# Mixture of experts: the weights of the routes travel with the scattered rows, and the gathers add to x by themselves

## The chip, the cores and the metric

The kernel runs on one core of a Trainium2 chip. A core has a matrix engine (PE, with a queue of its own for loading weights, PEld), a vector engine (DVE), a scalar engine (ACT), GpSimd (POOL) and SyncE (SP); SP and POOL issue the data transfers (DMAs) here, which run on 16 DMA engines. The metric is the device time in microseconds (us) of one execution. Lower is better.

## The reference

The model has two pre-norm transformer blocks over 8 sequences of 512 tokens with 256 features each, in float32:

```
x = x + attn0(layernorm(x));  x = x + ffn0(layernorm(x))
x = x + attn1(layernorm(x));  x = x + ffn1(layernorm(x))
```

- attn0: 16 query heads over 4 key and value heads of 16 features, rotary positions, causal. attn1: 16 heads of 16 with biases, causal.
- ffn0: a router picks 8 of 32 experts for each token, with the softmax weights divided by their sum over the eight; ffn1: 2 of 16, with the softmax weights as they are, plus a shared expert of inner width 352 for every token. An expert is `h = silu(x @ wg) * (x @ wu)`, and the token's result adds `(h @ wd) * w_e`. The inner width is 96 in ffn0 and 176 in ffn1.

Since the weight w_e is one number for a token and an expert, `(h @ wd) * w_e` and `(h * w_e) @ wd` are the same up to rounding.

## The kernel before

A token's row of x lives in a tile `x` of 128 partitions with 4 x 256 floats: token 128 t + p of a sequence is on partition p in part t. Only four such tiles are in the core's memory at once, so between its stages a sequence's x goes out to DRAM (`x_after`, L161) and is fetched again (`fetch_x`, L164).

**Order of the stages.** Attention 0 over the eight sequences (0 to 676 us of the profile), layer 0's experts (676 to 1172), attention 1 (1172 to 1768), layer 1's experts (1768 to 2003), and a tail that puts out the last three sequences (2003 to 2056). In the attention stages a sequence's layer norm (L289), router (`route`, L313) and, in layer 1, the shared expert run beside the attention of the next one (`pipeline`, L743).

**Sorting by expert.** For each layer and part of the sequences (layer 0: sequences 0 to 3 and 4 to 7; layer 1: 0 to 4 and 5 to 7) DRAM holds a slab `xg` (L222) with room for each expert's tokens one after the other. `route` finds each token's experts, its weights `wt` (one column for each expert, zero where it isn't chosen, L350 to L357) and its row in each chosen expert's part of the slab. An indirect DMA on POOL for each t and each of the k choices then scatters 128 normed rows of 256 floats (L384): 32 for a sequence in layer 0, and 8 in layer 1. Three wide DVE instructions after them (L394, L397, L399) bring the weights into the order of the choices, as `lay.weights`.

**Experts.** `tables` (L980) works out, at run time, which tiles of 128 rows there are and to which expert each belongs; `registers` (L1076 to L1096) reads that into registers of SP (where a tile's rows begin) and PE (where the expert's weights lie), eight tiles at a time. `experts` (L1068) then runs over pairs of tiles, 150 in layer 0 and 44 in layer 1, in five stages with lags of 0, 4, 5, 6 and 7 steps (L1172): load the rows (L1106, six buffers), transpose them on PE and copy to xT (L1115, L1117), the gate and up products with silu on ACT and one multiply on DVE (L1132, L1137 to L1141), transpose h (L1151, L1152), the down product (L1162), a copy on ACT (L1167) and a store into a second slab `yg` (L1168). PE's order is the one in which the program writes it (L1173). The other engines' order within their queues is set by a scheduler of the framework.

**Gathers.** When all tiles of a part are stored, indirect DMAs on POOL gather a token's results from `yg` (L1199), 32 for a sequence in layer 0 and 8 in layer 1, 128 rows of 256 floats each. They land in a ring of four tiles of two gathers each (`AHEAD`, `PART`), and for each of them DVE computes x = g * weight + x (`add`, L1210). The gathers of layer 0's sequences 0 to 3 run beside the second part of its experts (`x_in_ring`, L1366), and those of 4 to 7 beside attention 1, two sequences ahead (`ahead1`, L1438). In layer 1, sequences 0 to 4 are gathered and put out beside the second part (`results`, L1279), and 5 to 7 in the tail, with a ring of eight tiles. `Beside` (L1046) hands such work out between the steps of the experts. `behind` orders an add after DVE's latest copy of an expert's h, or after the latest mask in attention 1, so that adds don't overtake these.

Of the kernel before, what the change touches and what calls it, by code (L numbers as in the profile page):

```python
# [72 lines left out]
AHEAD = 4  # L73
# [18 lines left out]
def two_blocks_kernel(  # L92
# [56 lines left out]
    zeros = cpool.tile([P, D], F32, tag="zeros", name="zeros")  # L149
# [60 lines left out]
    class Layer:  # L210
        def __init__(self, n, part, seqs, n_e, k, gu):
# [10 lines left out]
            self.xg = drp.tile([n_e * self.cap + P, D], F32, tag=f"xg{name}", name=f"xg{name}")  # L222
# [16 lines left out]
            self.weights = routes("weights", k, F32)  # L239
# [41 lines left out]
    def layernorm(x, lnp, name, tag="xn", bufs=1):  # L281
# [7 lines left out]
        xn = lnp.tile([P, NT, D], F32, tag=tag, name=f"xn_{name}", bufs=bufs)  # L289
        for t in range(NT):  # L290
            nc.vector.tensor_scalar(
                xn[:, t, :], x[:, t, :], mv[:, t, 0:1], rstd[:, t : t + 1], ALU.subtract, ALU.mult
            )
# [18 lines left out]
    def ffn_parts(smp, bank):  # L312
        def route(n, b, xn, xT, name, again):  # L313
# [36 lines left out]
            wt = smp.tile([P, NT, n_e], F32, tag="wt", name=f"wt_{name}")  # L350
# [31 lines left out]
            for t in range(NT):  # L382
# [7 lines left out]
            yield  # L390

            same = smp.tile([P, NT, k, n_e], F32, tag="same", name=f"same_{name}", bufs=1)
            shape = [P, NT, k, n_e]
            nc.vector.tensor_tensor(  # L394
                same, key.unsqueeze(2).to_broadcast(shape), keys[:, :, :k].unsqueeze(3).to_broadcast(shape), ALU.is_equal
            )
            nc.vector.tensor_tensor(same, same, wt.unsqueeze(2).to_broadcast(shape), ALU.mult)  # L397
            weights = lay.weights[b]
            nc.vector.tensor_reduce(weights, same, AX.X, ALU.add)  # L399
# [580 lines left out]
    def tables(lay, small, bank, again, beside=None):  # L980
# [3 lines left out]
        lay.offi = tpool.tile([1, 2, most], I32, tag=f"offi{lay.part}", name=f"offi{name}")[:, :, :n_t]  # L984
# [41 lines left out]
        offf = small.tile([1, 2, n_t], F32, tag="offf", name=f"offf_{name}", bufs=1)  # L1026
        dn = D if lay.n == 0 else ND1 * D
        nc.vector.tensor_scalar(offf[:, 0, :], ex, float(n_e - 1), float(lay.gu), ALU.min, ALU.mult)
        nc.vector.tensor_scalar(offf[:, 1, :], ex, float(n_e - 1), float(dn), ALU.min, ALU.mult)
# [3 lines left out]
        for lo in range(0, n_e, 8):  # L1033
            with tc.issue_after(beside.load) if beside else ExitStack():
# [5 lines left out]
                for rows in at:  # L1040
                    inst = nc.sync.dma_start(out=lay.xg[rows, :], in_=zeros)
                    tc.declare_no_dep(inst.ins, group=group, reason="these rows are no token's")
                    tc.add_to_no_dep_group(group, inst.ins)
            yield

    class Beside:  # L1046


        def __init__(self, *items):
# [3 lines left out]
            self.last = None  # L1053
# [17 lines left out]
    def experts(n, gu, dn, mp, ps, again, beside):  # L1071
# [10 lines left out]
        def registers(lay, i):  # L1082
# [7 lines left out]
                    lay.offi[0:1, j, i : min(i + RB, lay.tiles(again))], engines=[ENG.PE], min_val=0, max_val=(lay.n_e - 1) * step,  # L1090
                    skip_runtime_bounds_check_because="an expert's number is at most the last one's",
                )[1]
                for j, step in enumerate((lay.gu, w_dn))
# [6 lines left out]
        def load(lay, i):  # L1100
# [3 lines left out]
            xg = mp.tile([P, 2, D], F32, tag="xg", name=f"xg_{name}_{part}_{i}", bufs=6)  # L1104
# [4 lines left out]
        def turn_x(lay, i):  # L1109
            part = lay.part  # L1110
            xg = made.pop(("xg", part, i))
# [8 lines left out]
        def gate_up(lay, i):  # L1120
            part = lay.part
            xT = made.pop(("xT", part, i))
# [4 lines left out]
            else:  # L1127
                gus = [ps.tile([P, 2 * inner], F32, tag="gu", name=f"gu_{name}_{part}_{i + j}") for j in range(2)]
            for j in range(2):
# [6 lines left out]
                if n:  # L1136
                    nc.scalar.activation(h[:, j, :], gus[j][:, :inner], AF.Silu)  # L1137
                    nc.vector.tensor_tensor(h[:, j, :], h[:, j, :], gus[j][:, inner:], ALU.mult)
            if n == 0:
                nc.scalar.activation(h, whole[:, :, :inner], AF.Silu)  # L1140
                nc.vector.tensor_tensor(h, h, whole[:, :, inner:], ALU.mult)  # L1141
            made["h", part, i] = h

        def turn_h(lay, i):
# [7 lines left out]
            beside.last = nc.vector.tensor_copy(hT[: chunks[0][1]], hp[: chunks[0][1]]).ins  # L1152
# [28 lines left out]
    PART = 2  # L1181

    def gathers(n, b, gat, again=""):
# [11 lines left out]
        for t in range(NT):  # L1195
            for lo in range(0, k, PART):
                g = gat.tile([P, PART, D], F32, tag="gath", name=f"g{name}_{t}_{lo}")
                for i in range(PART):
                    nc.gpsimd.indirect_dma_start(  # L1199
                        out=g[:, i, :], out_offset=None, in_=lay.yg[: lay.tiles(bool(again)) * P, :],  # L1200
                        in_offset=bass.IndirectOffsetOnAxis(ap=rows[:, t, lo + i : lo + i + 1], axis=0),
                    )
                yield b, t, lo, g, lay.weights[b]

    def add(part, behind):

        b, t, lo, g, weights = part
        with tc.issue_after(behind()) if behind() else ExitStack():
            for i in range(PART):
                nc.vector.scalar_tensor_tensor(  # L1210
                    xs[b][:, t, :], g[:, i, :], weights[:, t, lo + i : lo + i + 1], xs[b][:, t, :], ALU.mult, ALU.add
                )

    def gathered(n, b, gat, again="", behind=lambda: None):

        wait = []
        made = gathers(n, b, gat, again)
        while True:
            if len(wait) == AHEAD:
                add(wait.pop(0), behind)  # L1220
            part = next(made, None)
            if part is None:
                break
            wait.append(part)
            yield
        while wait:
            add(wait.pop(0), behind)
            yield
# [475 lines left out]
```

## Time and profile before

| | us |
|---|---|
| median of three runs | 2077.69 (2077.26 to 2086.83) |
| profiled execution | 2057.66 |
| its span | 2055.8 |
| PE busy in it | 1619.5 (79%) |
| DVE busy | 1088.5 (53%) |
| ACT busy | 649.2 (32%) |
| POOL busy | 645.7 (31%) |

The profile is of one execution. A line of the page's groups reads: line of the program, engine, operation, what it writes <- what it reads, count | busy time in all (us), mean of one (ns) | idle time of the engine just before them and what ended it most. A line of the windows gives a stretch of time and how long each engine was busy in it. In a timeline, the bracket at a line's end is how long the engine stood idle before it, and what released it: "issue" is time in which it waited for nothing that the profile shows, "remote" is a releaser that the profile cannot name. Waits are given as engine, output and line <- what it waited for: us in total, how often, the longest.

### The profile page before, as it was taken

The numbers are of one execution on the slowest core, as the hardware profiler recorded it, in microseconds if no ns is written. First come the engines' busy times: TensorE is split into PE (matmuls) and PEld (weight loads), VectorE is DVE, ScalarE is ACT, GpSimd is POOL, SyncE is SP. The second block draws the span as 40 slices with busy tenths as digits, with TensorE's granted clock in tenths as the row PEclk, the third lists the DMA queues.
The fourth block names the chain that finished last, engine by engine and source line by source line (L and its number), as shares of the span: only waits on it lengthen the run. The fifth ranks groups of instructions, "written<-read, shape, count | busy, mean of one in ns | idle before, by whom it ended". The sixth has DMA issues, their size and how long they took to land.

```text
span 2055.8 us, 31001 instructions
## 1 busy us (share of the span) xinstructions
PE 1619.5 (79%) x10180; PEld 1070.6 (52%) x10180; DVE 1088.5 (53%) x3311; ACT 649.2 (32%) x867; POOL 645.7 (31%) x662
## 2 busy tenths in 40 slices
PE   5967467477533799997988989788897998999892
PEld 3424234233212699987877735444443545677671
DVE  5657256266342444445766546667566554543352
ACT  3524234234210233322222254343342454122121
POOL 0052452442565000015444301545444111100434
PEclk9978688687775899999999999898998998999995
DMA  1123233321224567667777500332332212443454
GB/s 60 40 93 85 85 95 106 127 73 57 93 97 151 159 224 229 188 186 209 219 213 215 171 8 22 111 113 72 111 101 63 79 42 70 151 144 114 136 172 136
DMA packets 230552, 247.73 MB, mean 121 GB/s; under 512 B 80212, under 2 KB 203220, under 8 KB 230388
## 3 DMA queue, kind: packets, MB, share of 16 engines
q1 hardware_dynamic: 199172, 160.88, 25.8%
q0 software_dynamic: 30720, 83.93, 12.8%
q8 instruction: 89, 1.46, 0.3%
q10 hardware_dynamic: 496, 0.85, 0.1%
q14 instruction: 75, 0.61, 0.1%
HBM read 127.06 MB, written 118.49 MB: 119 GB/s over the span
## 4 chain that ended last, share of the span: by engine, by line
PE 58%; another core or an unknown queue 8%; DVE 8%; issue 6%; ACT 2%; DMA 1%; ACTq 0%; SPq 0%; DVEq 0%
PE gu_m L1132 14%; PE y_m L1162 10%; PE st_a L647 5%; PE xgT_m L1115 4%; PE o_a L670 4%; PE hT_m L1151 3%; PE sg_f L411 2%; PE sy_f L424 2%; PE su_f L411 2%; PE q_a L963 2%; PE y_a L736 2%; PE lg_f L320 1%; PE k_a L968 1%; PE v_a L950 1%
## 5 line engine op out<-in xcount | busy, mean ns | idle before, releaser
L1199 POOL DMA_INDIRECT g<-yg,yrows x320 | 315.5, 986 | 705.0 <-DMA xg_m<-xg 231.2
L384 POOL DMA_INDIRECT xg<-xn_f,rows_f x320 | 325.3, 1017 | 671.5 <-DVE rows_f L381 336.6
L652 ACT ACTIVATE p_a<-st_a 128x2048 f32<-128x2048 f32 (+1 forms) x192 | 305.9, 1593 | 434.6 <-PE st_a L647 228.9
L1132 PE MATMUL gu_m<-gw,xgTs_m 128*128 x1552 | 348.6, 370 | 28.5 <-DVE xgTs_m L1117 14.5
L647 PE MATMUL st_a<-qT_a,kT_a 32*128 32x512 f32 (+3 forms) x2048 | 214.4, 504 | 122.4 <-ACT p_a L652 68.4
L1132 PEld LDWEIGHTS gu_m<-gw,xgTs_m 128*128 128x128 f32 x1552 | 268.4, 199 | 60.9 <-issue 19.9
L1162 PE MATMUL y_m<-dw,hTs_m 96*128 (+1 forms) x952 | 244.8, 388 | 1.5 <-DVE hTs_m L1152 1.5
L670 PE MATMUL o_a<-p_a,v 128*32 128x512 f32 (+3 forms) x2048 | 206.3, 479 | 18.6 <-DVE p_a L658 11.8
L658 DVE TENSOR_TENSOR p_a<-p_a,causal 128x512 f32<-128x512 f32 x256 | 170.3, 682 | 87.5 <-ACT p_a L652 70.3
L647 PEld LDWEIGHTS st_a<-qT_a,kT_a 32*128 32x128 f32 x2048 | 95.1, 200 | 228.4 <-issue 107.9
L1117 DVE COPY xgTs_m<-xgT_m 128x512 f32<-128x512 f32 x194 | 133.5, 688 | 147.7 <-PE xgT_m L1115 102.4
L1167 ACT COPY ys_m<-y_m 128x512 f32<-128x512 f32 x194 | 113.6, 585 | 239.9 <-PE y_m L1162 148.9
L1162 PEld LDWEIGHTS y_m<-dw,hTs_m 96*128 96x128 f32 (+1 forms) x952 | 170.0, 195 | 18.3 <-DVE hTs_m L1152 1.8
L1152 DVE COPY hTs_m<-hT_m 96x256 f32<-96x256 f32 (+1 forms) x194 | 92.7, 478 | 129.2 <-PE hT_m L1151 85.7
L1115 PE MATMUL xgT_m<-ident,xg_m 128*128 128x128 f32 x776 | 122.8, 281 | 17.6 <-DMA xg_m<-xg 12.6
L1140 ACT ACTIVATE h_m<-gu_m 128x192 f32<-128x192 f32 x150 | 49.5, 331 | 254.4 <-PE gu_m L1132 142.7
L1210 DVE SCALAR_TENSOR_TENSOR x_a<-g,weights,x_a 128x256 f32<-128x256 f32 x256 | 122.1, 477 | 4.1 <-issue 0.6
L670 PEld LDWEIGHTS o_a<-p_a,v 128*32 128x32 f32 x2048 | 52.2, 113 | 137.8 <-issue 88.7
L1115 PEld LDWEIGHTS xgT_m<-ident,xg_m 128*128 128x128 f32 x776 | 99.1, 145 | 42.3 <-issue 17.0
L1151 PE MATMUL hT_m<-ident,h_m 128*96 128x128 f32 (+1 forms) x476 | 87.4, 282 | 40.8 <-DVE h_m L1141 19.4
L676 DVE COPY osb_a<-o_a 128x512 f32<-128x512 f32 x64 | 43.9, 687 | 137.1 <-remote 93.2
L736 PE MATMUL y_a<-wo,oT_a 128*128 128x256 f32 x256 | 75.1, 431 | 39.4 <-ACT oT_a L729 37.7
(203 smaller groups left out, 1775.5 us busy)
## 6 DMA issues: line engine op xcount, KB each, us to landing
xg_m<-xg SPq DMA_DIRECT2D x388, 128.0 KB
yg<-ys_m SPq DMA_DIRECT2D x194, 256.0 KB
xg<-zeros SPq DMA_DIRECT2D x100, 128.0 KB
xg<-xn_f,rows_f POOLq DMA_INDIRECT x320
g<-yg,yrows POOLq DMA_INDIRECT x320
xf<-in_x_dram SPq DMA_DIRECT2D x8, 512.0 KB
x_after<-x_in SPq DMA_DIRECT2D x8, 512.0 KB
x_a<-x_after SPq DMA_DIRECT2D x8, 512.0 KB
```

The costliest lines, as they stand in the source:

```text
L384: inst = nc.gpsimd.indirect_dma_start(out=lay.xg, out_offset=bass.IndirectOffsetOnAxis(ap=rows[:, t, i : i + 1], axis=0), in_=xn[:, t, :], ...
L647: nc.tensor.matmul(st[:, g, at : at + T - j * P], kT[r, j * P : (j + 1) * P], qT[r, j * P :], start=True, stop=True,)
L652: nc.scalar.activation(pt, st[:, :, :width], AF.Exp, scale=SCALE)
L658: self.masked = nc.vector.tensor_tensor(d, d, causal.unsqueeze(1).to_broadcast([P, NG, P]), ALU.mult).ins
L670: nc.tensor.matmul(o[32 * g : 32 * g + 32, j * P :], v1[:, j, v_at + g * (DH + 1) :][:, :32], probs[n][:, g, at : at + T - j * P], start=( ...
L1115: nc.tensor.transpose(tr[:, j, c, :], xg[:, j, c * P : (c + 1) * P], ident)
L1117: nc.vector.tensor_copy(xT, tr)
L1132: nc.tensor.matmul(gus[j], xT[:, j, c, :], gu[:, bass.ds(at + c * 2 * inner, 2 * inner)], start=(c == 0), stop=(c == ND - 1),)
L1151: nc.tensor.transpose(hp[:n_in, q, j, :], h[:, j, lo : lo + n_in], ident)
L1162: nc.tensor.matmul(y[:, j, :], hT[:n_in, q, j, :], dn[:n_in, bass.ds(at + q * D, D)], start=(q == 0), stop=(q == n_ch - 1),)
L1199: nc.gpsimd.indirect_dma_start(out=g[:, i, :], out_offset=None, in_=lay.yg[: lay.tiles(bool(again)) * P, :], in_offset=bass.IndirectOffset ...
L1210: nc.vector.scalar_tensor_tensor(xs[b][:, t, :], g[:, i, :], weights[:, t, lo + i : lo + i + 1], xs[b][:, t, :], ALU.mult, ALU.add)
```

## The change

The weight of a token for an expert is no longer applied when the results are added to x, but between the expert's two products. For this the slab `xg` has rows of 256 + n_e floats (288 in layer 0, 272 in layer 1): the normed tile gets n_e spare columns, `route` writes the weights of all experts into them, and the same 32 or 8 indirect DMAs scatter them with the row. The loads of the experts' tiles are as much wider, and their tiles are held one stage longer, in seven buffers for six. In `gate_up` DVE multiplies silu(gate) by the token's weight and by up in one instruction for each tile, where layer 0 had one for each pair without a weight. Which of the spare columns holds the weight depends on the tile's expert, so DVE now reads the experts' numbers into registers as well.

The results in `yg` can then be added as they are. A gather becomes an indirect DMA that adds to x, without a tile between them, and DVE's additions are gone, with the ring of tiles and the orders that `behind` set. For each sequence the gathers go round the four t first and then to the next choice, so one that adds to a part of x comes four after the one that added to it before, and has to wait until that one has landed. The x tile must have been fetched before its first gather. Beside layer 0's experts all four sequences are fetched before the first gather is issued. The three DVE instructions that ordered the weights by choice are gone too.

```diff
-            self.xg = drp.tile([n_e * self.cap + P, D], F32, tag=f"xg{name}", name=f"xg{name}")
+            self.width = D + n_e
+            self.xg = drp.tile([n_e * self.cap + P, self.width], F32, tag=f"xg{name}", name=f"xg{name}")
...
-        xn = lnp.tile([P, NT, D], F32, tag=tag, name=f"xn_{name}", bufs=bufs)
+        xn = lnp.tile([P, NT, D + spare], F32, tag=tag, name=f"xn_{name}", bufs=bufs)
...
-            wt = smp.tile([P, NT, n_e], F32, tag="wt", name=f"wt_{name}")
+            wt = xn[:, :, D : D + n_e]
...
-            same = smp.tile([P, NT, k, n_e], F32, tag="same", name=f"same_{name}", bufs=1)
-            shape = [P, NT, k, n_e]
-            nc.vector.tensor_tensor(
-                same, key.unsqueeze(2).to_broadcast(shape), keys[:, :, :k].unsqueeze(3).to_broadcast(shape), ALU.is_equal
-            )
-            nc.vector.tensor_tensor(same, same, wt.unsqueeze(2).to_broadcast(shape), ALU.mult)
-            weights = lay.weights[b]
-            nc.vector.tensor_reduce(weights, same, AX.X, ALU.add)
...
-        nc.vector.tensor_scalar(offf[:, 0, :], ex, float(n_e - 1), float(lay.gu), ALU.min, ALU.mult)
-        nc.vector.tensor_scalar(offf[:, 1, :], ex, float(n_e - 1), float(dn), ALU.min, ALU.mult)
+        for i, step in enumerate((lay.gu, dn, 1)):
+            nc.vector.tensor_scalar(offf[:, i, :], ex, float(n_e - 1), float(step), ALU.min, ALU.mult)
...
-                for j, step in enumerate((lay.gu, w_dn))
+                for j, (eng, step) in enumerate(((ENG.PE, lay.gu), (ENG.PE, w_dn), (ENG.DVE, 1)))
...
-            xg = mp.tile([P, 2, D], F32, tag="xg", name=f"xg_{name}_{part}_{i}", bufs=6)
+            xg = mp.tile([P, 2, lay.width], F32, tag="xg", name=f"xg_{name}_{part}_{i}", bufs=7)
...
+            def scaled(j):
+
+                nc.vector.scalar_tensor_tensor(
+                    h[:, j, :], h[:, j, :], xg[:, j, D:][:, bass.ds(offs[part, i + j][2], 1)], gus[j][:, inner:],
+                    ALU.mult, ALU.mult,
+                )
...
-                    nc.vector.tensor_tensor(h[:, j, :], h[:, j, :], gus[j][:, inner:], ALU.mult)
+                    scaled(j)
             if n == 0:
                 nc.scalar.activation(h, whole[:, :, :inner], AF.Silu)
-                nc.vector.tensor_tensor(h, h, whole[:, :, inner:], ALU.mult)
+                for j in range(2):
+                    scaled(j)
...
-        for t in range(NT):
-            for lo in range(0, k, PART):
-                g = gat.tile([P, PART, D], F32, tag="gath", name=f"g{name}_{t}_{lo}")
-                for i in range(PART):
-                    nc.gpsimd.indirect_dma_start(
-                        out=g[:, i, :], out_offset=None, in_=lay.yg[: lay.tiles(bool(again)) * P, :],
-                        in_offset=bass.IndirectOffsetOnAxis(ap=rows[:, t, lo + i : lo + i + 1], axis=0),
-                    )
-                yield b, t, lo, g, lay.weights[b]
-
-    def add(part, behind):
-
-        b, t, lo, g, weights = part
-        with tc.issue_after(behind()) if behind() else ExitStack():
-            for i in range(PART):
-                nc.vector.scalar_tensor_tensor(
-                    xs[b][:, t, :], g[:, i, :], weights[:, t, lo + i : lo + i + 1], xs[b][:, t, :], ALU.mult, ALU.add
+        for i in range(k):
+            for t in range(NT):
+                nc.gpsimd.indirect_dma_start(
+                    out=xs[b][:, t, :], out_offset=None, in_=lay.yg[: lay.tiles(bool(again)) * P, :],
+                    in_offset=bass.IndirectOffsetOnAxis(ap=rows[:, t, i : i + 1], axis=0), compute_op=ALU.add,
                 )
+                if t % 2:
+                    yield
...
             def x_in_ring():
                 for b in range(SPLIT[0]):
                     fetch_x(b, x_after[0], f"a1{g}")
-                    yield from gathered(0, b, gat, g, behind)
+                yield
+                for b in range(SPLIT[0]):
+                    yield from gathers(0, b, gat, g)
...
-                beside.add(done, end, SPLIT[0] * 21, x_in_ring())
+                beside.add(done, end, SPLIT[0] * 16 + 1, x_in_ring())
             else:
-                beside.add(done, end, SPLIT[1] * 10, results(range(SPLIT[1]), gat, gat, ps, g, behind))
+                beside.add(done, end, SPLIT[1] * 6, results(range(SPLIT[1]), gat, gat, ps, g))
```

## The prediction

> **What bounds the kernel now.** I read the page first (busy shares and slices), then windows by stage, then the chain of waits for POOL, then the timeline around POOL's bursts. The page and its groups:
>
> ```profile
> PE 1619.5 (79%) x10180; PEld 1070.6 (52%) x10180; DVE 1088.5 (53%) x3311; ACT 649.2 (32%) x867; POOL 645.7 (31%) x662
> L1199 POOL DMA_INDIRECT g<-yg,yrows x320 | 315.5, 986 | 705.0 <-DMA xg_m<-xg 231.2
> L384 POOL DMA_INDIRECT xg<-xn_f,rows_f x320 | 325.3, 1017 | 671.5 <-DVE rows_f L381 336.6
> L1210 DVE SCALAR_TENSOR_TENSOR x_a<-g,weights,x_a 128x256 f32<-128x256 f32 x256 | 122.1, 477 | 4.1 <-issue 0.6
> ```
>
> PE is the bound (79%); DVE, where the change saves, is at 53%. Windows (start:end, us, then busy us of PE, PEld, DVE, ACT, POOL, granted clock, DMA share, GB/s) show where PE does not work:
>
> ```profile
> 676.00:904.00 228.00, 220.40 (x1372) 203.22 (x1373) 111.85 (x271) 69.42 (x153) 0.00 (x0) 0.97 0.66 202
> 904.00:1172.00 268.00, 230.07 (x1304) 205.29 (x1302) 161.54 (x410) 65.86 (x147) 125.98 (x130) 0.92 0.70 207
> ...
> 1294.00:1375.00 81.00, 69.13 (x443) 34.78 (x442) 53.28 (x167) 31.91 (x29) 41.73 (x41) 0.89 0.33 96
> 1912.00:1953.00 41.00, 33.40 (x145) 24.29 (x144) 13.76 (x30) 7.46 (x18) 23.13 (x24) 0.88 0.50 143
> ```
>
> The first two are the halves of layer 0's experts: without gathers PE idles 7.6 of 228 us, with 128 gathers 37.9 of 268. The others are one sequence's 32 gathers in attention 1 (PE idle 11.9 of 81) and gathers in layer 1's experts (7.6 of 41). Next, one sequence's 32 scatters in attention 0, cut in four, and four such bursts whole:
>
> ```profile
> 117.00:127.00 10.00, 9.11 (x84) 3.57 (x82) 9.46 (x22) 5.39 (x8) 8.04 (x7) 1.00 0.33 100
> 127.00:137.00 10.00, 3.81 (x36) 1.75 (x32) 4.79 (x20) 2.15 (x2) 7.57 (x9) 0.73 0.36 132
> 137.00:147.00 10.00, 4.25 (x18) 1.22 (x18) 0.69 (x1) 1.02 (x1) 7.56 (x9) 0.50 0.28 101
> 147.00:159.00 12.00, 0.00 (x0) 0.00 (x0) 0.00 (x0) 0.00 (x0) 9.26 (x10) 0.50 0.30 108
> 117.00:159.00 42.00, 17.18 (x134) 6.54 (x132) 14.94 (x42) 8.56 (x10) 32.42 (x32) 0.67 0.32 110
> 192.00:235.00 43.00, 16.00 (x122) 6.50 (x120) 15.66 (x46) 8.22 (x10) 32.18 (x32) 0.67 0.32 110
> 433.00:476.00 43.00, 18.64 (x139) 7.71 (x142) 15.02 (x42) 10.14 (x10) 32.62 (x32) 0.69 0.28 98
> 507.00:550.00 43.00, 22.66 (x163) 10.32 (x162) 13.65 (x26) 10.33 (x10) 32.65 (x32) 0.78 0.27 95
> ```
>
> This is the reading that carries the forecast. While POOL issues indirect DMAs without a pause, the others run on for some 10 us, then trickle, then stop until the burst ends: PE does 18.6 us of work in 42.8 (mean of the four), 24.1 idle. It happens with scatters and, shorter, with gathers. POOL's timeline, its waits, and what ACT was doing meanwhile:
>
> ```profile
> 912.22 0.95 POOL L1199 DMA_INDIRECT g<-yg,yrows  x1 [0.30 <-issue]
> 913.47 0.94 POOL L1199 DMA_INDIRECT g<-yg,yrows  x1 [0.30 <-issue]
> 925.22 0.95 POOL L1199 DMA_INDIRECT g<-yg,yrows  x1 [10.80 <-DVE x_a L1210]
> ```
>
> ```profile
> POOL g L1199 <- DVE x_a L1210: 149.3, 33, 17.4
> ```
>
> ```profile
> 916.07 0.33 ACT L1140 ACTIVATE h_m<-gu_m 128x192 f32<-128x192 f32 x1 [6.50 <-remote]
> ```
>
> One gather costs POOL 0.95 + 0.30 = 1.25 us. In experts 0 it gets through eight, ACT stands 6.50 us for something the profile cannot name, and it resumes after the burst. The burst ends only because the ring of four gather tiles is full and POOL must wait for DVE's add. Bursts of six or fewer show no stall. So that wait, 33 times, keeps gathers in harmless groups. The change removes it.
>
> **The change part by part.** Sums are against the profiled execution's 2057.66 us (span 2055.8 and 1.9 around it); the median of the runs, 2077.69, is 20.0 above that, and I add 20 at the end.
>
> 1. *Adds L1210 gone*: 320 x 0.477 = 153 us of DVE. DVE is no bound (161.5 of 268 where most of them lie), PE is: worth 0 beside what the gathers do. In the tail the last add (0.48 us) and its neighbours go from the path: about -1.
>
> 2. *Weights by expert gone* (L394 to L399): 3.65 us of DVE per sequence in attention 0 (1.217 + 1.217 + 1.209), 0.84 in attention 1. They run inside the scatter burst, in its first 10 us, whose length POOL sets (32 x 1.26 = 40 us). Idle after that is not shortened, but 3.65 us come free for useful work: at most 8 x 3.65 = -29, at least 0; near 0, since DVE does only 14 to 16 us in such a burst and then has nothing: **-5**.
>
> 3. *Scaling in gate_up* (L1138, L1141): per pair of tiles one 0.341 us multiply becomes two of half the width with a scalar each, and DVE reads experts' numbers into registers. The nearest rows are L1210 itself (0.477 for 256 wide with a scalar per partition) and DVE's register load L1531 (0.547). Per pair at most 2 x 0.38 - 0.34 = +0.42, and 0.55/4 = 0.14; 194 pairs. DVE does 0.69 + 0.34 + 0.42 = 1.45 us of a pair's 2.83, so it is covered. Without cover it would be 194 x 0.35 = +68; ACT's silu to PE's turn of h has 1.25 us of slack (ready 908.90, used 910.15), and 0.35 fits: **0**.
>
> 4. *Wider rows*: layer 0 loads grow by 1/8 of 128 KB, layer 1's by 1/16; scatters likewise, zeros too. By its packets (1,024 B, 46 ns) the loads take 0.22 of the 0.70 DMA share in experts 0: +0.03. xg is loaded four stages ahead and now has seven buffers for the one stage longer that it is held: **0**.
>
> 5. *Gathers as accumulating DMAs.* POOL issues as many (320 x 1.25 us), but a gather now waits for x to be loaded (for experts 0 all four sequences are, at 416.8 to 682.5 us) and for the earlier gather into the same rows, four before it, to land. Four gathers take POOL 5.0 us. Plain gathers land a median 3.2 us after their issue begins in experts 0 (nine in ten within 3.8, none over 4.4), 2.4 to 2.7 elsewhere, by their packets; at the tail the first gather starts at 2011.90 and its add at 2014.61, 2.7 us. An accumulating one is in no row. Its bounds: 2.4 us (the add is free) and about 6.4 (everything twice). I take 4, near the plain rows, since only the data part, not the completion, should double. 4 is under 5.0: the chain never holds POOL, and with DVE's adds gone nothing else does. Queued behind a waiting gather on POOL are only gathers, and scatters in attention 1.
>
> The Trainium skill, "DMA: Bandwidth & Descriptors", section "Anatomy of one DMA — SWDGE (gpsimd) path", fits 2.0 us plus bytes at 436 GB/s: 2.3 us for 128 KB, under this trace's 2.4 to 3.2. "Collectives: The Full Stack", section "The bandwidth ceiling: the fold count and why AG ≠ RS ≠ AR", says an add needs two source reads and so halves the rate; an estimate by both is 2.6 us, on the same side of 5.0, so this rule speaks against the change, and the sum by it is the same.
>
> So gathers come as unbroken bursts, priced by the scatter windows above:
> - *Experts 0*: rows are computed from 585 us on, so all 128 issue from 904.66 on: 128 x 1.25 = 160 us. PE has 230 us of work left at 904. It does 10 in the first 10 us, then 0.30 of the time (mean share of the four bursts after their first ten: (18.6 - 9)/32.8): 150 x 0.30 = 45, so 55. The rest, 175, follows: 904 + 160 + 175 = 1239 against 1172, **+67**. Ends: at the whole bursts' share 18.6/42.8 PE does 70, +52; if the stop of the last 12 us persists, 19, +103.
> - *Attention 1*: four bursts of 40 us. Idle 24.1 against 11.9 is +12.2; if the remaining 50.5 us of work still run at 0.93 ((528.5 - 4 x 69.1) of (596 - 4 x 81) us, attention 1 outside these windows), 43 + 54 - 81 = +16.4. Between: 4 x 14 = **+57** (49 to 66).
> - *Experts 1*: 32 at a stretch, then 8: 24.1 - 7.6 = **+16** (10 to 25).
> - *Tail*: 24 gathers, 30 us, the same set of them: **+1** (-1 to +12, the landing).
>
> Sum: -5 + 67 + 57 + 16 + 1 = +136: 2194, median **2214** (A; its own range 2150 to 2290).
>
> What starves the engines is not settled. The trace's instruction-loading queue moved 89 packets, 1.46 MB, and shows none between 514.7 and 556.8 us, over one scatter burst; so late instruction loads are the likely cause. The Trainium skill, "Runtime: NRT & Kernel Launch", section "Terms", has instruction memory refilled in 16 KiB blocks; that fits the packets, and says nothing of POOL delaying them. If POOL's own stream runs dry in 128 gathers, the long burst breaks, which is the +52 end.
>
> **The rivals.**
> - *B, throttled only where DMA is busy.* In experts 0 (share 0.70) landing passes 5 us, gaps open, PE keeps about its pace there; attention 1 and experts 1 starve as in A. -5 - 5 + 57 + 16 + 1 = +64: 2142. For it: landing is 0.8 us longer there already. Against: it needs 2 us more.
> - *C, the other side: the chain paces POOL.* Where an accumulating gather lands later than 6.0 us everywhere, each four are followed by a gap of 1 us or more, and groups of four stall nothing. Then PE's idle falls to that without gathers: experts 0, 37.9 to 8: -30; attention 1, 11.9 to 0.073 x 81 = 5.9, four times: -24; experts 1: -6; attention 0: -5; tail, three more waits of 1 to 3 us: +6. -59: 1999, median 2019. For it: twice the slowest plain landing exceeds 6. Against: it needs almost twice the median.
> - *E, far slower landing.* Over 9.5 us each, 8 rounds of 4 are 76 us, so in attention 1 x arrives after the next sequence wants it: about 10 us by each of four at 12 us and more in the tail (6 waits of 7): 2078 + 80 = 2160 and up to 2400 at 20 us.
> - *Nothing, since DVE hid it all*: needs gathers to keep their grouping without the adds; nothing is left that would do that.
>
> **How the numbers follow.** A .47, B .14, C .28, E .08, nothing .03. A measurement of this kernel tells about 0.5% (10 us) from no change. Faster takes C; same, the last and the edges of C; slower A, B and E. The range must reach from C to A's top: 2005 leaves out the lower part of C (.1), 2290 the top of A and most of E (.1).
>
> **What would show it.** A: POOL in experts 0 with gathers 1.25 us apart for over 100 us, waiting "issue" 0.30, while PE, ACT and DVE show long "remote" waits and PE's slices fall below 5; attention 1 with four holes of 20 us or more; DVE's total down by 153 + 36 less the new scaling. Wrong if POOL's gathers show waits of over 1 us every four (C), if bursts of gathers longer than 12 let PE run (then all of part 5 is worth 0 to -60), or if the waits for DVE's h grow in experts (part 3).

## The result, and the profile after

The changed kernel takes 2327.15 us (median; 2325.53 to 2330.71), the kernel before 2079.34 beside it: a ratio of 1.119, with a 95% interval of 1.116 to 1.122. The profiled execution took 2330.71 us (span 2329.0), 273 more than that of before; the forecast had 136 more.

The page of the changed kernel, its first line and four of its groups:

```profile
PE 1603.4 (69%) x10180; PEld 1061.8 (46%) x10180; DVE 963.4 (41%) x3097; ACT 649.4 (28%) x865; POOL 818.4 (35%) x662
...
L384 POOL DMA_INDIRECT xg<-xn_f,rows_f x320 | 316.6, 989 | 800.4 <-DVE rows_f L381 456.2
L1193 POOL DMA_INDIRECT x_a<-yg,yrows x256 | 398.2, 1555 | 372.2 <-DMA xg_m<-xg 231.0
...
L1121 DVE SCALAR_TENSOR_TENSOR h_m<-h_m,xg_m,gu_m 128x96 f32<-128x96 f32 (+1 forms) x388 | 114.7, 326 | 106.5 <-ACT h_m L1134 64.2
L286 DVE BATCH_NORM_STATS2 stats_a<-x_a 128x6 f32<-128x256 f32 x32 | 13.5, 422 | 342.4 <-DMA x_a<-yg,yrows 342.4
```

DVE is 125 us less busy, and nobody profits. A gather costs POOL 1.56 us for 0.99. The last line is the one to find: 32 instructions of 0.42 us, the layer norm's statistics, stood 342 us at DVE's head, waiting for gathers. In the profile of before the same 32 cost no wait worth naming:

```profile
L286 DVE BATCH_NORM_STATS2 stats_a<-x_a 128x6 f32<-128x256 f32 x32 | 13.2, 412 | 0.2
```

The waits of the changed kernel, and one of them in the timeline:

```profile
DVE stats_a L286 <- DMA x_a<-yg,yrows: 342.4, 24, 59.7
```

```profile
1004.82 0.43 DVE L286 BATCH_NORM_STATS2 stats_a<-x_a 128x6 f32<-128x256 f32 x1 [59.71 <-DMA x_a<-yg,yrows]
...
1012.26 0.68 DVE L1106 COPY xgTs_m<-xgT_m 128x512 f32<-128x512 f32 x1
...
1013.00 2.29 PE L1129 MATMUL gu_m<-gw,xgTs_m 128*128 x6 [64.52 <-DVE xgTs_m L1106]
```

DVE stands 59.71 us for sequence 0's last gathers. Behind it in DVE's queue is the copy of an expert's x, and PE stands 64.52 us for that copy. In attention 1 it happens with each of the four sequences. The windows (columns as in the prediction):

```profile
936.00:1173.00 237.00, 82.51 (x467) 73.98 (x465) 54.75 (x169) 23.60 (x52) 197.92 (x128) 0.66 0.70 130
1130.00:1173.00 43.00, 40.33 (x244) 37.16 (x244) 23.34 (x66) 12.01 (x27) 35.98 (x24) 0.93 1.01 235
1173.00:1303.00 130.00, 130.00 (x824) 120.74 (x823) 71.35 (x184) 42.70 (x93) 1.92 (x3) 1.00 0.72 205
1424.00:1485.00 61.00, 16.86 (x135) 9.96 (x127) 8.96 (x29) 8.96 (x8) 50.17 (x32) 0.66 0.58 86
2186.00:2260.00 74.00, 73.67 (x366) 56.62 (x364) 29.18 (x56) 20.61 (x49) 61.71 (x40) 1.00 0.87 192
```

The 128 gathers of experts 0 are one unbroken burst, as forecast (at 1.85 us each, 237 us), and PE works 82.5 us in it. So far this could be the forecast's starving. But the second line is the last 43 us of the same burst, after the third sequence's statistics: POOL still issues 24 gathers, no statistics wait for them, and PE works 40.33 us. And the last line is a burst of 40 gathers in layer 1's experts, as unbroken, in which PE works 73.67 of 74 us: no layer norm waits for those either. By stage, with borders at the first transposition of an expert's tile and the last down product of each layer:

| us | before | after | difference | forecast |
|---|---|---|---|---|
| attention 0 | 642 | 666 | +24 | -5 |
| experts 0 | 529 | 637 | +108 | +67 |
| attention 1 | 600 | 723 | +123 | +57 |
| experts 1 | 237 | 242 | +5 | +16 |
| tail | 48 | 61 | +12 | +1 |

### The profile page after: what moved, and what is told of

It is laid out like the page before. It is cut to its first block, busy times and chain, and to the rows that moved or that the text cites. A ratio compares the mean times of both kernels' runs of the same rounds, so it can differ in the third digit from the quotient of the medians.

```text
span 2329.0 us, 30887 instructions
## 1 busy us (share of the span) xinstructions
PE 1603.4 (69%) x10180; PEld 1061.8 (46%) x10180; DVE 963.4 (41%) x3097; ACT 649.4 (28%) x865; POOL 818.4 (35%) x662
## 3 DMA queue, kind: packets, MB, share of 16 engines
q0 software_dynamic: 61440, 88.65, 18.6%
## 4 chain that ended last, share of the span: by engine, by line
PE 55%; POOL 14%; another core or an unknown queue 10%; issue 8%; DVE 5%; ACT 3%; DMA 2%; SPq 1%; DVEq 0%; ACTq 0%; POOLq 0%
POOL x_a L1193 13%; PE gu_m L1129 12%; PE y_m L1160 8%; PE st_a L637 6%; PE o_a L660 5%; PE xgT_m L1104 3%; ACT p_a L642 3%; PE hT_m L1149 2%; PE y_a L726 2%; PE sy_f L414 2%; PE qkv_a L842 2%; PE su_f L401 2%; PE sg_f L401 2%; PE q_a L953 1%
## 5 line engine op out<-in xcount | busy, mean ns | idle before, releaser
L384 POOL DMA_INDIRECT xg<-xn_f,rows_f x320 | 316.6, 989 | 800.4 <-DVE rows_f L381 456.2
L1193 POOL DMA_INDIRECT x_a<-yg,yrows x256 | 398.2, 1555 | 372.2 <-DMA xg_m<-xg 231.0
L1129 PE MATMUL gu_m<-gw,xgTs_m 128*128 x1552 | 342.7, 365 | 124.0 <-DVE xgTs_m L1106 119.7
L307 PE MATMUL xT_f<-ident,xn_f 128*128 128x128 f32 x128 | 26.7, 329 | 228.2 <-DVE xn_f L291 228.2
L1193 POOL DMA_INDIRECT x_c<-yg,yrows x64 | 98.7, 1543 | 199.0 <-DVE hTs_m L1150 165.3
L1121 DVE SCALAR_TENSOR_TENSOR h_m<-h_m,xg_m,gu_m 128x96 f32<-128x96 f32 (+1 forms) x388 | 114.7, 326 | 106.5 <-ACT h_m L1134 64.2
L286 DVE BATCH_NORM_STATS2 stats_a<-x_a 128x6 f32<-128x256 f32 x32 | 13.5, 422 | 342.4 <-DMA x_a<-yg,yrows 342.4
L307 PEld LDWEIGHTS xT_f<-ident,xn_f 128*128 128x128 f32 x128 | 16.8, 154 | 242.4 <-issue 230.1
```

The costliest lines, as they stand in the source:

```text
L384: inst = nc.gpsimd.indirect_dma_start(out=lay.xg, out_offset=bass.IndirectOffsetOnAxis(ap=rows[:, t, i : i + 1], axis=0), in_=xn[:, t, :], ...
L1121: nc.vector.scalar_tensor_tensor(h[:, j, :], h[:, j, :], xg[:, j, D:][:, bass.ds(offs[part, i + j][2], 1)], gus[j][:, inner:], ALU.mult, A ...
L1129: nc.tensor.matmul(gus[j], xT[:, j, c, :], gu[:, bass.ds(at + c * 2 * inner, 2 * inner)], start=(c == 0), stop=(c == ND - 1),)
L1193: nc.gpsimd.indirect_dma_start(out=xs[b][:, t, :], out_offset=None, in_=lay.yg[: lay.tiles(bool(again)) * P, :], in_offset=bass.IndirectOf ...
```

## The experiments

Two theories stood against each other. **W**: the time is lost in DVE's queue. **S**, the forecast's: POOL's unbroken issue starves the engines. The runs came in five groups, each on one chip with the kernel before beside it. The kernel before took 2054, 1710, 1710, 2075 and 1714 us in them; where it took some 1710, the scatters' holes in attention 0 were absent (from the profiles of a1, a2, a3 and e7 below). I call these quiet groups and the others starving ones; the first measurement above was in a starving one too. The third and the fourth group ran on the same chip, one quiet and one starving, so it is not the chip alone. Ratios are taken within a group; where two groups are set side by side, the text says so.

### DVE's queue mended (e1_stats_late; starving)

```diff
-            nc.vector.tensor_copy(hT[: chunks[0][1]], hp[: chunks[0][1]])
+            hT_last[0] = nc.vector.tensor_copy(hT[: chunks[0][1]], hp[: chunks[0][1]]).ins
...
-            xn = layernorm(x, lnp, name)
+            with tc.issue_after(att.masked or hT_last[0]):
+                xn = layernorm(x, lnp, name)
```

> The changed kernel, with one order added on DVE: the layer norm of attention 1 (its first instruction is the statistics, L286) may not be queued before the last copy of an expert's h (sequences 0 and 1) or before the latest mask of the attention (the others). Nothing is left out. Theory W (DVE's queue): the time comes from statistics that stand at the head of DVE's queue and wait for the last gather into their x, with the experts' and the softmax's work behind them: 59.7 + 37.6 + 3.0 + 38.4 = 139 us of DVE's waits in experts 0 and four holes of PE of 48 us in attention 1. Then this run loses about 139 + 4 x 46 = 320 us against the changed kernel: 1990 to 2060. Theory S (the forecast's: unbroken issue by POOL starves the other engines): POOL issues as before, so PE stays empty in those bursts, and the time stays within 40 us of 2327.

Measured: 2034.66 us against 2054.12, a ratio of 0.992 (0.988 to 0.995). One edit that adds an order and removes no work turns 12% slower into 0.8% faster. The waits and the window of the same burst:

```profile
DVE stats_a L286 <- DMA x_a<-yg,yrows: 44.2, 16, 8.6
```

```profile
923.00:1160.00 237.00, 215.24 (x1319) 194.61 (x1317) 121.92 (x339) 68.44 (x148) 197.58 (x129) 0.96 1.03 245
```

Same POOL, same 237 us, and PE does 215 us of work in them instead of 82.5. W holds; S falls for these gathers, in a group where the scatters' holes are there.

### Plain gathers in the same program (e2_plain_stats_late; starving)

```diff
                     in_offset=bass.IndirectOffsetOnAxis(ap=rows[:, t, i : i + 1], axis=0),
-                    compute_op=ALU.add,
```

> As e1_stats_late, but the gathers write x instead of adding to it, so x after a layer's experts is the last gathered row alone (the sum over the experts and the residual are left out). POOL then issues a gather every 1.25 us, as in the kernel before, 128 of them without a break. Theory S: PE falls below half of its time over 160 us of experts 0, 50 us or more above e1_stats_late. Theory W: nothing waits on the burst, PE stays above 0.85 in it, and the time is that of e1_stats_late or up to 20 us less. The accumulating gathers' POOL time against the plain ones' (1.55 against 0.95 us) is to be seen on POOL's lines.

Measured: 2297.53 us in one run, 263 more than e1_stats_late, 159 of them in experts 0. (From layer 1's router on it computes with another x; experts 0's burst lies ahead of that.) The burst whole, and its part after 10 us:

```profile
931.00:1091.00 160.00, 28.76 (x113) 23.07 (x112) 8.49 (x23) 4.59 (x10) 121.23 (x128) 0.56 0.43 124
931.00:941.00 10.00, 7.87 (x51) 7.09 (x49) 2.86 (x8) 1.51 (x3) 7.64 (x8) 1.00 0.79 228
941.00:1091.00 150.00, 20.89 (x62) 15.98 (x63) 5.63 (x15) 3.08 (x7) 113.59 (x120) 0.53 0.41 117
```

So S is real, for gathers that come every 1.25 us: PE does 20.9 us of work in 150 (0.14 of the time, where the forecast took 0.30), and no layer norm is at the head: DVE has no wait for gathers in this run. In the changed kernel an accumulating gather takes POOL longer:

```profile
1001.26 0.95 POOL L1196 DMA_INDIRECT x_a<-yg,yrows  x1 [0.30 <-issue]
1002.51 0.95 POOL L1196 DMA_INDIRECT x_a<-yg,yrows  x1 [0.30 <-issue]
```

```profile
945.61 1.54 POOL L1193 DMA_INDIRECT x_a<-yg,yrows  x1 [0.30 <-issue]
947.46 1.53 POOL L1193 DMA_INDIRECT x_a<-yg,yrows  x1 [0.31 <-issue]
```

The first two lines are this run's, the others the changed kernel's: 1.25 us against 1.85 from one to the next. That this pace is what spares the changed kernel is likely, not shown: an accumulating gather also moves its rows in other packets, and no run gave plain gathers a slower pace in a starving group.

### Parts 1 to 4 alone (e3_scaled_only, starving; g4_scaled_only_again, starving)

The changed kernel with the gathers, the ring and DVE's adds of before, the add without a weight:

```diff
-        for i in range(k):
-            for t in range(NT):
-                nc.gpsimd.indirect_dma_start(out=xs[b][:, t, :], ..., compute_op=ALU.add)
+        (the gathers into tiles of the kernel before)
...
+                nc.vector.tensor_tensor(xs[b][:, t, :], xs[b][:, t, :], g[:, i, :], ALU.add)
```

> Parts 1 to 4 of the change alone: weights scattered with the rows, wider rows, h scaled by DVE; the gathers and DVE's adds are those of the kernel before (a ring of four tiles, adds ordered behind the experts' copies), the add without its weight. Both theories: the gathers make the difference, so this stays within 15 us of the kernel before (2079), a little below for the 3.65 us of DVE less per sequence in attention 0. If the scaling were not covered, as in part 3's other end, +68: 2147. If the 29 us that attention 0 is longer in the changed kernel come from the wider scatters or the order of the program, they show here: 2100.

> e3_scaled_only once more (parts 1 to 4 with the old gathers and adds). Where the kernel before takes 1710 and nothing starves: if the 1.6% came from where starved bursts fall, 0.995 to 1.005; if the wider rows or the scaling cost by themselves, 1.012 to 1.02. Where it takes 2054: 1.016 again.

Measured: 1.016 (1.012 to 1.019) and 1.012 (1.007 to 1.017). The first is more than the 15 us expected, and like the case in which a loss shows in attention 0. Nearly all of it is in attention 0 (against the profile of before, which is of another starving group): experts 0 began at 666 and 669 us, where before has 642; experts 0 then took 530 and 535 us, where before has 529. The scaling is covered, as forecast; its instruction takes 305 ns per tile in layer 0, twice that against one of 341 before:

```profile
L1123 DVE SCALAR_TENSOR_TENSOR h_m<-h_m,xg_m,gu_m 128x96 f32<-128x96 f32 x300 | 79.8, 305 | 38.4 <-issue 20.0 <-ACT h_m L1139 13.6 <-ACT ys_m L1167 3.1
```

Whether the loss in attention 0 is there in a quiet group, the second run did not tell, since it fell into a starving one.

### Wider rows alone (a2_wide_only; quiet)

```diff
+            self.width = D + n_e
-            self.xg = drp.tile([n_e * self.cap + P, D], F32, ...)
+            self.xg = drp.tile([n_e * self.cap + P, self.width], F32, ...)
...
-            wt = smp.tile([P, NT, n_e], F32, tag="wt", name=f"wt_{name}")
+            wt = xn[:, :, D : D + n_e]
```

> The kernel before with the weights written into the normed rows and scattered with them, and the loads as wide as in the changed kernel; the weights by choice, the gathers and DVE's adds stay those of before. e3_scaled_only, which also leaves out the three DVE instructions for the weights by choice, was 1.6% slower than the kernel before, nearly all in attention 0 (experts 0 began at 666 us for 642). If the wider rows or the weights' place are the cause, this is 1.2 to 1.9% slower; if it is the program's order without the three instructions, within 0.5%.

Measured: 1715.25 against 1709.68, 1.003 (1.000 to 1.006). The wider rows cost next to nothing where nothing starves. Whether they are the cause of the loss in attention 0 that e3_scaled_only had in a starving group, this run cannot say.

### The changed kernel in a quiet group (a1_changed_again)

No edit.

> The changed kernel itself, unaltered, once more beside others. The kernel before took 2054 us on one chip and 1710 on another, where 32 scatters at 1.29 us left PE at 0.93. Where the kernel before takes some 2054 to 2079 us, 1.12 times that, as before: 2300 to 2330. Where it takes some 1710, the scatters' holes are gone, but DVE's queue is the same: the waits of 139 us in experts 0 and 4 x 46 us in attention 1 stay, and the time is 1710 + 250 to 330: 1960 to 2040, a ratio of 1.15 to 1.19. If DVE's waits came only with the starved engines, 1710 to 1830.

Measured: 2047.41 against 1709.68, 1.198 (1.191 to 1.205), just above the expected range. The scatters leave PE alone here (40.36 us of work in the 43 of the first burst), and DVE's wait is what it was:

```profile
117.00:160.00 43.00, 40.36 (x351) 20.93 (x350) 35.50 (x127) 23.35 (x24) 33.36 (x32) 1.00 0.55 168
661.00:897.00 236.00, 81.92 (x453) 73.20 (x453) 53.66 (x163) 23.10 (x51) 197.24 (x128) 0.65 0.70 129
```

```profile
DVE stats_a L286 <- DMA x_a<-yg,yrows: 341.9, 24, 59.9
```

The loss is 338 us, DVE's waits are 342, and S is not needed for it. Against a3_short_pause_again below, which is as fast as the kernel before in the same group, the stages differ by -22 (attention 0: 424 for 446), +161, +169, +14 and +12 us. So where nothing starves, taking the three DVE instructions away does shorten attention 0, by 22 of at most 29 us (a2_wide_only, of the same group, keeps the three and has 446); in a starving group the same edit went with 24 us more.

### The two places apart (g1_stats_late_again, g2_late_experts_only; starving)

g1 is e1_stats_late again. g2 puts the layer norms behind the last copy of an expert's h only:

```diff
-            with tc.issue_after(att.masked or hT_last[0]):
+            with tc.issue_after(hT_last[0]):
                 xn = layernorm(x, lnp, name)
```

> e1_stats_late once more (the layer norm of attention 1 queued late on DVE). On a chip where the kernel before takes some 1710 us: the changed kernel's 2047 less DVE's 342 us of waits for gathers would be 1705; the accumulating gathers take POOL 0.6 us more each, which binds attention 1 (40 DMAs, 72 us a sequence, where PE needs 64 to 68) and the tail (+12): 1740 to 1800, a ratio of 1.02 to 1.05. If mending DVE's queue brought all back: 1.00. Where the kernel before takes 2054: 0.99, as before.

> The changed kernel with the layer norms of attention 1 queued behind the last copy of an expert's h, but no later: the three waits in experts 0 go, the four in attention 1 stay. By the waits, 139 us of 342 go: on a chip with 1710 for the kernel before, 2047 - 139 = 1908 (1880 to 1930); with 2054 to 2079, 2327 - 139 = 2188 or somewhat less.

Measured against 2075.47: g1 2045.96, 0.986 (0.982 to 0.989); g2 2199.74, 1.060 (1.055 to 1.065). DVE's waits for gathers in the two:

```profile
DVE stats_a L286 <- DMA x_a<-yg,yrows: 44.4, 16, 8.5
```

```profile
DVE stats_a L286 <- DMA x_a<-yg,yrows: 191.5, 12, 45.9
```

The first is g1's, the second g2's (four sequences at some 48 us); g2 came out a little above the 2188 expected. From the changed kernel's 1.119, which is of another starving group, to g2's 1.060 are 0.059 of 2075, 122 us, for experts 0, and on to g1's 0.986, in the same group, 154 us, for attention 1: 276 us for 298 us of waits taken away (342 less 44). By e1_stats_late's ratio of 0.992 it is 0.127 of 2054, 261 us.

### The pace of the scatters (e4_scatter_pause, g3_half_pause, starving; e7_short_pause, a3_short_pause_again, h2_scatter_pause_again, quiet)

The kernel before with a fill of a scratch tile on POOL after each of layer 0's scatters, 512, 256 or 64 columns wide:

```diff
                     tc.add_to_no_dep_group(group, inst.ins)
+                    if n == 0:
+                        with tc.issue_after(inst.ins):
+                            nc.gpsimd.memset(pause, 0.0)
```

> The kernel before, with a fill of a scratch tile of 128x512 on POOL after each of layer 0's scatters, so that a scatter comes every 1.6 to 2 us instead of 1.26. If an unbroken issue at 1.26 us is what stops PE in attention 0's bursts, the pauses let it run: PE above 0.8 in the bursts, and up to 8 x 20 us less, 1920 to 2000. If each scatter holds the others by itself, or the burst's length counts, the holes last as long as the longer burst: 8 x 15 to 25 us more, 2200 to 2280.

> e4_scatter_pause with a fill of 128x256 for 128x512: a scatter every 1.42 us or so. Where the kernel before takes 1710: 256 x 1.42 = 364 us of POOL in attention 0, just below what PE needs there, so 0.995 to 1.01. Where it takes 2054: 0.90 if 1.42 us is slow enough, 0.95 to 1.0 if most holes stay.

> e4_scatter_pause with a fill of 128x64 for 128x512: about 0.1 us for 0.54, so that a scatter comes every 1.25 to 1.4 us. If the rate of issue decides, most of the holes stay: 1980 to 2054. If any other instruction between two scatters is enough, it is as fast as e4_scatter_pause or faster, since the bursts are shorter: 1830 to 1870.

> e7_short_pause once more, which told nothing on a chip where the kernel before has no holes. Where the kernel before takes some 2054 us or more: if the rate of issue decides, most of the holes stay with 1.29 us for 1.26, 1980 to 2054 (0.96 to 1.0 of the kernel before); if another instruction between two scatters is enough, as good as the longer fill or better, 0.89 to 0.91.

> e4_scatter_pause once more. Where the kernel before takes 2054 or more: 0.903 again. Where it takes 1710: POOL binds attention 0 at 1.7 us a scatter (436 us for the 256, where they take 373 with the short fill), 1.03 to 1.04.

| | from one scatter to the next | group | ratio to the kernel before |
|---|---|---|---|
| 64 wide | 1.29 us | quiet, twice | 1.001 (0.999 to 1.004), both times |
| 256 wide | 1.46 us, now and then 1.62 | starving | 0.926 (0.921 to 0.932) |
| 512 wide | 1.68 us | starving | 0.903 (0.899 to 0.907) |
| 512 wide | 1.68 us | quiet | 1.011 (1.007 to 1.015) |

The first burst of e4_scatter_pause, which the kernel before did with 17.18 us of PE in the same 42:

```profile
117.00:159.00 42.00, 37.80 (x297) 18.91 (x296) 35.33 (x98) 21.12 (x22) 37.69 (x48) 0.92 0.46 135
```

And that of a3_short_pause_again, at 1.29 us in a quiet group:

```profile
117.00:160.00 43.00, 39.84 (x307) 19.88 (x306) 35.54 (x114) 20.60 (x20) 38.07 (x64) 0.92 0.52 157
```

In a starving group fills that slow the pace of one engine's DMAs make the whole kernel 10% faster (202 us, more than the 160 expected at most); some 1.5 us is most of the way, between the two cases expected of g3. With the long fill attention 0 takes 466 us in the starving group (e4_scatter_pause) and in the quiet one (h2_scatter_pause_again), so its holes are gone. Experts 0 and attention 1, whose plain gathers have no fills, still take 497 and 602 us in the one and 443 and 545 in the other. The short fill met no starving group, so whether any instruction in between would do stays open. With the long fill POOL binds attention 0, which costs 1.1% where nothing starves, less than the 3 to 4% expected.

### Both mended, and the gathers paced too (e5_late_and_pause, e6_scaled_pause, e8_plain_paused, a4_pause_everywhere, h1_pause_everywhere_again; all quiet)

e5 is e1_stats_late with the 512-wide fill after every scatter, e6 e3_scaled_only with it after layer 0's, e8 e2_plain_stats_late with it after every gather. a4, and h1 again, are the kernel before with it after every scatter and gather. All five fell into quiet groups, where there is nothing to cure.

> e1_stats_late with a fill of 128x512 on POOL after every scatter, in layer 1 too. If the two holes are two causes (DVE's queue; scatters issued at 1.26 us), their gains add: 2035 - 202 (what e4_scatter_pause gained against the kernel before) = 1833, and up to 40 less, since PE's gaps of 10 to 12 us where eight scatters follow 32 gathers in attention 1 go as well: 1790 to 1840. If they share a cause, it stays above 1852.

> e3_scaled_only with the pauses of e4_scatter_pause (layer 0's scatters). e3_scaled_only was 1.6% (32 us) slower than the kernel before, mostly in attention 0. If parts 1 to 4 cost only by where attention 0's holes fall, this is within 8 us of e4_scatter_pause's ratio of 0.903: 0.898 to 0.908. If the scaling in the experts or the wider rows cost by themselves, it keeps 15 to 32 us over it: 0.911 to 0.920.

> e2_plain_stats_late (gathers that write x, the sum over the experts and the residual left out) with a fill of 128x512 after each gather. If plain gathers starve the engines by their rate, a period of 1.7 us is as harmless as the accumulating gathers' 1.85: PE above 0.85 in experts 0's burst and 2020 to 2060 in all. If plain gathers do so whatever their rate, it stays near 2297 or above.

> The kernel before with a fill of 128x512 after every scatter and every gather of both layers. Where the kernel before takes some 2054 us: 0.903 of it as e4_scatter_pause, and some 38 - 8 = 30 us of PE's gaps in experts 0 and 4 x 6 in attention 1 less: 0.875 to 0.90. Where it takes some 1710: attention 0's bursts are bounded by POOL at 1.7 us (256 x 1.7 = 436 us for 373), 1.02 to 1.05.

> a4_pause_everywhere once more. Where the kernel before takes 2054 us or more: e4_scatter_pause's 0.903, less 30 us of PE's gaps beside gathers in experts 0 and 24 in attention 1, 0.875 to 0.895, if plain gathers starve PE by the same rate as scatters; 0.903 or above if not. Where it takes 1710: 1.049 again.

Measured, against 1710.11 (e5, e6, e8), 1709.68 (a4) and 1713.52 (h1): e5 1821.05, 1.064 (1.060 to 1.069); e6 1764.79, 1.031 (1.027 to 1.035); e8 1717.80, one run; a4 1793.07 and h1 1794.64, 1.049 both. What they can say: e6 shows DVE's queue at work in another place. Its second `tables` starts with an instruction (L982) that stands for the slower scatters, and the experts' work stands behind it:

```profile
DVE count L982 <- DMA xg<-xn_f,rows_f: 40.1, 1, 40.1
```

That is about what e6 has over h2_scatter_pause_again's 1.011, of another quiet group (0.020 of 1710, 34 us); h2 has no such wait. Second, with POOL paced in such a way, POOL becomes the bound; in e5 a sequence's 32 gathers and 8 scatters fill 72 us of attention 1, and PE has 58.73 us of work in them:

```profile
1066.00:1138.00 72.00, 58.73 (x403) 31.10 (x403) 38.08 (x124) 30.33 (x28) 60.65 (x45) 0.92 0.57 100
```

What they can't: whether the gains of e1_stats_late and e4_scatter_pause add in a starving group, whether pauses cure the plain gathers' holes there (e8 was meant for that), and, since e5 has the pauses as well, what the mended change costs or gains in a quiet one. No version was found that beats the kernel before in both kinds of group: e4_scatter_pause is 9.7% faster in one and 1.1% slower in the other.

## Why the prediction was wrong

The direction was right by luck: all of the forecast loss was starving by gathers, and that did not occur. The size (2214, at most 2290, for 2327) and the mechanism were wrong. One of the forecast's own signs of being wrong came true, too: bursts of more than 12 gathers that let PE run (40 in layer 1's experts, 128 in e1_stats_late). By its steps:

1. *Adds gone: worth 0.* As a saving, yes. But the adds were also what kept DVE's queue in order: in the program of before, a sequence's statistics stand behind the adds into the same x, and these were spread between the experts' copies. Without them the framework's scheduler put sequence 0's statistics behind the multiply of the seventh pair of the second part. This is the step that failed, with the sentence in step 5 that asked who is queued behind a waiting gather, and looked at POOL alone. The first reader of what a gather writes is on DVE, in order, with the experts' and the softmax's work behind it. No rival had it either. Shown by e1, g1, g2 and a1.
2. *Weights by choice gone, -5.* Measured -22 in a quiet group and +24 in a group with holes, where the wider rows came with it. The bound of -29 was good; why the holes cost more without the three instructions was not settled.
3. *Scaling, 0* and 4. *wider rows, 0.* Right: experts 0 took 530 us for 529 with both; wider rows alone 1.003, in a quiet group.
5. *Accumulating gathers.* The landing was right in size: by their packets a median of 3.5 us in the changed kernel and 5.2 in e1_stats_late's experts 0, where the loads run beside (taken as 4, at most 6.4). Four gathers take POOL 7.4 us, so the chain never holds it, and rivals B, C and E fall. (The estimate from the Trainium skill's pages "DMA: Bandwidth & Descriptors", section "Anatomy of one DMA — SWDGE (gpsimd) path", and "Collectives: The Full Stack", section "The bandwidth ceiling: the fold count and why AG ≠ RS ≠ AR", 2.6 us, was under both; the measurement decides.) The unbroken burst was right. POOL's price was wrong: "as many, 320 x 1.25 us" were 1.85 us each, since an accumulating gather takes POOL 1.56 us for 0.99. I bounded its landing from both sides and its issue not at all. At that pace nothing starved (PE worked 215 of 237 us in e1_stats_late), so of the +140 us for starving nothing came true here. With plain gathers every 1.25 us it did: e2_plain_stats_late took 263 us more. There the share of 0.30 was too high as well (0.14).
6. *Tail, +1.* +12: 24 gathers at 1.85 us are 44 us where they were 30.

So the forecast missed a loss of some 260 to 276 us, counted one of 140 that does not occur, and came out low. Its reading of the scatters' holes in the kernel before was right, and is worth 9.7% of that kernel in a starving group.

What starves the engines is still only argued. In the quiet changed kernel three instruction loads of 16 KB arrive in each of the first three scatter bursts; in the profile of before one arrives in each of the first six, within 8 us of the burst's start, and none after. That fits late loads, but an engine that stands for another reason would ask for none either. And 8 KB packets of the second queue that the profile calls instruction do arrive in the bursts of before, one 39 us after the first burst's start, so not everything of that kind is held up.

## What to carry to other kernels

An instruction that waits for a DMA also keeps its engine's queue in order; when the DMA takes its work over, look for the next reader of that data, on which engine it sits, and what a scheduler puts behind it. An order that adds no work (statistics after the copies, and in attention 1 after the masks) was worth some 260 to 276 us here. Where engines stand for something the profile calls remote, look at what another engine issues meanwhile, and try it slower.

## What was not expected of the hardware

An accumulating indirect gather of 128 rows of 1 KB takes POOL 1.56 us and lands in a median of 3.5 us, a plain one 0.95 and 2.4 (e2). The DMA packets of the software queue are twice as many (61440 in e1, 30720 in e2 for the same bytes). And the same kernel takes 1710 or 2050 to 2080 us, by the group of runs. Bursts of 32 scatters at 1.26 us stop the other engines in the one and not in the other, and are the largest part of it: attention 0 takes 446 us in a3 (quiet) for 642 in the profile of before, experts 0 443 for 529, attention 1 549 for 600. The traces do not show what differs between the groups.
